# The last projection of a two-layer cross-attention with tokens on partitions: one kernel before and after the change

## The chip, the cores and the metric

The kernel runs on one core of one Trainium2 chip, in fp32. A core has five engines with instruction streams of their own: PE (TensorE, matrix products into PSUM), DVE (VectorE), ACT (ScalarE), POOL (GpSimd) and SP (SyncE, which here only issues DMA transfers). Each engine takes its instructions in order, and semaphores hold an instruction until what it needs from another engine or from a transfer is there. So an instruction that waits also holds everything behind it on its engine. The metric is the device time in microseconds, the median of several runs.

## What is computed

Two cross-attention layers, one after the other, on 8 batches of 100 tokens with 1024 features (`x`); each batch has a context of 1444 rows with 512 features.

```python
# layer 0
Q = query @ Wq + bq;  K = key @ Wk + bk;  V = key @ Wv + bv
weights = softmax(Q @ K^T * 1024**-0.5, axis=-1)        # over the keys
x = query + (weights @ V) @ Wo + bo
# layer 1
q = x @ Wq + bq;  k = ctx @ Wk + bk;  v = ctx @ Wv + bv
w = softmax(q @ k^T * 1024**-0.5, axis=1)               # over the queries
y = w @ v + x
mu, var = mean(y, -1), var(y, -1)
out = (y - mu) * rsqrt(var + 1e-6) * gamma + beta
```

In layer 1 the softmax runs over the query axis, so the weights of one query don't sum to one, and the bias `bv` enters a token's row multiplied by the sum of that token's weights. The kernel calls this sum `r`.

## The kernel before

**Layout.** The running activations are `xT`: features on partitions (8 chunks of 128) and all 800 tokens along the free dimension. Each layer forms, per batch, scores s with keys on partitions (12 chunks of 128, the last of 36 rows), the softmax, and A = context rows weighted by the softmax (512 features by 100 tokens). Values are never formed per key: A is projected afterwards by the value weights (`wv1`, 512 by 1024, in layer 1).

**What sets the order.** `alternated(b, ...)` (L1317) interleaves, on PE, the weighted rows A of batch b with the scores of batch b + 2, one step of each at a time: 48 steps, counted by n. When the scores of a batch are complete, its softmax (`softmax1`, L1128) is given out in pieces: DVE scales the scores and adds the key bias into `w`, takes the maximum over the tokens (`negmax`), ACT forms exponentials with their totals, DVE multiplies by the reciprocals, and POOL sums the weights over the keys (`weight_sums`, L1163). `LATER` says after how many pieces the rest of a softmax is put off until the next projection's code. DVE instructions between `vector.in_order = True` and `False` keep the order of the program; a scheduler places the others. The copy of a batch's A from PSUM to `A1T` is ACT's (L924).

**The second projection of layer 1.** `SETS` (L44) is batches 0 to 3, 4 to 6, and 7. After the A of a set's last batch, `project1` (L1197) multiplies with features on partitions: the weights are the stationary operand, the tokens (200 or 150 at a time) the moving one. It is a 2 by 2 block product with seven products in place of eight (X, Z, Y, W, reused and combined by additions); it needs four sums of weight blocks, made once by POOL (`project1_sums`, L1190), and four sums of token blocks, made by DVE for each set. Each product is 8 matmuls, and DVE adds the results into `xT`, where the residual already is.

**Finishing a batch.** `finish` (L1249) turns the batch's 100 columns of `xT` into token rows with 8 transposes on PE (`untransposed`, L1215 to L1232), DVE adds r times `bv` on the way out of PSUM into `z`, DVE takes mean and variance (`bn_stats`, `bn_aggr`), POOL raises the variance to -1/2, DVE forms (z - mean) * gamma, ACT scales, and POOL issues a transfer that adds `z` to the output, in which rows of beta have been written before: seven transfers by POOL (L1379) early in layer 1. `weight_totals` (L1179) gets r by transposing the sums of weights on PE and reducing on DVE. The dictionary `finished` (L1392) gives the batch and step n at which each is finished. `vectors` (gamma, beta and bv, repeated on all partitions, L1405 and after) are loaded after batch 3, into two of the ten buffers through which context tiles also stream.

**The end.** The last set is one batch. It is projected by `project_last` (L1263) with tokens on partitions in three pieces of columns; the first piece carries an extra column of row sums of the weights (`last_columns`, L1254, made by ACT), so that the mean is known early.

**Loads.** Context tiles (c, cT) come through SP's queue (`load_features`, `load_rows`), in the order of need, each when a buffer comes free.

Of the kernel before, what the change touches and what calls it, by code (L numbers as in the profile page):

```python
# [43 lines left out]
SETS = (range(0, 4), range(4, 7), range(7, 8))  # L44
LATER = {(1, 5): 4, (1, 7): 4}
# [10 lines left out]
def two_layer_cross_attention(ctx: ExitStack, tc: tile.TileContext, a: dict, out: bass.AP):  # L56
# [82 lines left out]
    prob = [feature_block(f"prob{n}") for n in range(3)]  # L139
    top = const.tile([P, P], F32, tag="top", name="top")  # L140
# [764 lines left out]
    def weighted_rows(s, layer, c, dst):  # L905
# [3 lines left out]
        for m in range(MC):  # L909
            r = max(keys(m), PAD)  # L910
            for k in range(LC):
                for h in both_sides():
                    nc.tensor.matmul(  # L913
                        ps[h * HP : (h + 1) * HP, k * T : (k + 1) * T],
                        c[m // CQ][:r, m % CQ, k * P + h * HP : k * P + (h + 1) * HP],
                        w[:r, m, :],
                        start=(m == 0 and k == 0),
                        stop=(m == MC - 1),
                        skip_group_check=True,
                    )  # L920
                if (m, k) == (MC - 1, LC - 1):
                    src = ps[:, :GT].rearrange("p (c t) -> p c t", t=T)
                    if layer:
                        nc.scalar.copy(dst, src)  # L924
                    else:
                        divided(s, ps, dst, src)
                yield

    def divided(s, ps, dst, src):
# [10 lines left out]
        r = work.tile([P, T], F32, tag="rrow", name=f"rrow_{s['b']}", bufs=2)  # L940
# [43 lines left out]
    def softmax0(s, groups, rest):  # L984
# [4 lines left out]
        most = work.tile([P, len(groups), T], F32, tag="most", name=f"most_{b}", bufs=1)  # L989
# [18 lines left out]
        shift = work.tile([P, P], F32, tag="shift", name=f"shift_{b}", bufs=1)  # L1008
# [154 lines left out]
    def weight_sums(s):  # L1163
# [4 lines left out]
        wsum = s["wsum"] = work.tile([P, T], F32, tag="wsum", name=f"wsum_{b}", bufs=6)  # L1168
# [10 lines left out]
    def weight_totals(pair):  # L1179

        n = P
        ps = bank(f"wsum_ps_{pair[0]['b']}")[:T, : 2 * n].rearrange("p (b n) -> p b n", n=n)
        for i, s in enumerate(pair):
            nc.tensor.transpose(ps[:, i, :], s["wsum"][:n, :], ident[:n, :n])
        r = small.tile([T, 2], F32, tag="r", name=f"r_{pair[0]['b']}", bufs=B // 2)
        nc.vector.tensor_reduce(r, ps, AX.X, ALU.add)
        for i, s in enumerate(pair):
            s["r"] = r[:, i : i + 1]

    def project1_sums(w):  # L1190
        t = weights.tile([P, LC, E], F32, tag="w", name="wv1_s")
        A = [[w[:, 2 * k + i, h * 512 : h * 512 + 512] for i in range(2)] for h in range(2) for k in range(2)]
        S = [[t[:, n, i * 512 : i * 512 + 512] for i in range(2)] for n in range(4)]
        left_sums(A, S, engine=nc.gpsimd)
        return A, S

    def project1(bs, A, S, At, between, room):  # L1197

        n, t0 = len(bs) * T // 2, bs[0] * T
        Bs = [[At[:, 2 * k + i, g * n : (g + 1) * n] for i in range(2)] for g in range(2) for k in range(2)]  # L1200
        sums = work.tile([P, LC, GT], F32, tag="gT", name=f"o1_{t0}_t", bufs=3).rearrange("p c t -> p (c t)")
        T_ = [[sums[:, (2 * k + i) * n : (2 * k + i + 1) * n] for i in range(2)] for k in range(4)]

        def add(r, g, banks):
            add_to_queries([4 * r + i for i in range(4)], t0 + g * n, n, banks)

        vector.in_order = True
        right_sums(Bs, T_)
        for _, steps in zip_longest(seven_products(f"o1_{t0}", A, Bs, S, T_, 4, n, add, add), room, fillvalue=0):
            for _ in range(steps):  # L1210
                next(between)
        run(between)
        vector.in_order = False

    def untransposed(s):  # L1215

        b = s["b"]  # L1220
        if b in range(3, 6):

            z = work.tile([P, LC, GT], F32, tag="gT", name=f"z_{b}", bufs=3).rearrange("p c t -> p (c t)")[:T, :E]
        else:
            z = row(f"z_{b}")[:T]
        s["z"] = z
        for j in range(2):
            ps = bank(f"z_{b}_{j}")
            for e in range(4):
                nc.tensor.transpose(ps[:T, e * P : (e + 1) * P], xT[:, 4 * j + e, b * T : (b + 1) * T], ident)  # L1230
            half = slice(j * 512, (j + 1) * 512)
            nc.vector.scalar_tensor_tensor(z[:, half], bv1[j][:T], s["r"], ps[:T, :], ALU.mult, ALU.add)  # L1232

    def normalise(s):
        b, z = s["b"], s["z"]
        stats = small.tile([T, 2, 6], F32, tag="stats", name=f"stats_{b}")
        for j in range(2):
            nc.vector.bn_stats(stats[:, j, :], z[:, j * 512 : (j + 1) * 512])
        mv = small.tile([T, 2], F32, tag="mv", name=f"mv_{b}")
        nc.vector.bn_aggr(mv, stats.rearrange("p a n -> p (a n)"))  # L1240
        rstd = small.tile([T, 1], F32, tag="rstd", name=f"rstd_{b}")
        nc.vector.tensor_scalar(rstd, mv[:, 1:2], EPS, None, ALU.add)
        nc.gpsimd.tensor_tensor(rstd, rstd, mhalf[:T], ALU.pow)  # L1243
        nc.vector.scalar_tensor_tensor(z, z, mv[:, 0:1], gamma[:T], ALU.subtract, ALU.mult)
        nc.scalar.activation(z, z, AF.Copy, scale=rstd)  # L1245

        nc.gpsimd.dma_start(out=out[b], in_=z, accum_op=ALU.add)

    def finish(s):  # L1249

        untransposed(s)
# [11 lines left out]
    def project_last(s, A, first):  # L1263
# [4 lines left out]
        z, centred = s["z"], row("centred")[:T]  # L1268
        n0 = first.shape[2] - 1
        parts = (slice(0, n0), slice(n0, n0 + 512), slice(n0 + 512, E))  # L1270
        unused = work.tile([P, L], F32, tag="half", name="unused", bufs=1)[:T]
        zs, sq = (small.tile([T, n], F32, tag=f"last{n}", name=f"last{n}") for n in (2, 3))
        mean, v, rstd = (small.tile([T, 1], F32, tag=n, name=n) for n in ("mean", "v", "rstd_last"))
# [4 lines left out]
        def scaled(part):  # L1278
            vector.tensor_tensor(z[:, part], centred[:, part], gamma[:T, part], ALU.mult)

        for j, part in enumerate(parts):
            n = part.stop - part.start
            ps = bank(f"ol_{j}")
            for k in range(LC):
                src = wv1[:, k, part] if j else first[:, k, :]
                m = src.shape[1]
                nc.tensor.matmul(ps[:T, :m], A[:, k, :T], src, start=(k == 0), stop=(k == LC - 1))
            if j == 0:
                vector.scalar_tensor_tensor(mean, ps[:T, n : n + 1], zs[:, 0:1], zs[:, 1:2], ALU.add, ALU.add)
                vector.tensor_scalar(mean, mean, 1.0 / E, None, ALU.mult)  # L1290
            vector.scalar_tensor_tensor(centred[:, part], ps[:T, :n], mean, z[:, part], ALU.subtract, ALU.add)
# [8 lines left out]
        nc.gpsimd.tensor_tensor(rstd, v, mhalf[:T], ALU.pow)  # L1300
        for half, queue in ((slice(0, E // 2), nc.sync), (slice(E // 2, E), nc.scalar)):
            vector.scalar_tensor_tensor(z[:, half], z[:, half], rstd, beta[:T, half], ALU.mult, ALU.add)
            queue.dma_start(out=out[B - 1][:, half], in_=z[:, half])
# [73 lines left out]
    for b in range(B - 1):  # L1377
        rows = a["L1_xattn_beta"].partition_broadcast(T)
        tc.keep_in_program_order(nc.gpsimd.dma_start(out=out[b], in_=rows))  # L1379
# [4 lines left out]
    cT = [list(load_features(0, parts=4)), list(load_features(1, (2,), 4))]  # L1384
    scores1 = scores_by_keys(batches[0], 1, cT[0], softmax1)
# [6 lines left out]
    finished = {(4, 2): 0, (4, 16): 1, (4, 30): 2, (5, 34): 3, (7, 2): 4, (7, 15): 5, (7, 28): 6}  # L1392
    totalled = {3: (0, 2), 6: (4,)}
    for bs in SETS:
        t = wide(f"A1T_{bs[0]}").rearrange("p c t -> p (c t)")[:, : LC * len(bs) * T]
        t = t.rearrange("p (c t) -> p c t", c=LC)
        for i, b in enumerate(bs):
            for n, _ in enumerate(alternated(b, 1, softmax1, t[:, :, i * T : (i + 1) * T])):
                if (b, n) in finished:
                    if (b, n) == (7, 28):  # L1400
                        weight_totals(batches[6:8])
                    finish(batches[finished[b, n]])
            if b == 1:
                AS = project1_sums(wv1)
            if b == 3:  # L1405
                vectors = [unit(f"vectors_{j}") for j in range(2)]
                gamma, beta = (v[:, :E] for v in vectors)
                bv1 = [v[:, E:] for v in vectors]
                for name, v in (("gamma", gamma), ("beta", beta)):
                    nc.gpsimd.dma_start(out=v, in_=a[f"L1_xattn_{name}"].partition_broadcast(P))  # L1410
                for j, v in enumerate(bv1):
                    nc.gpsimd.dma_start(out=v, in_=a["L1_xattn_bv"][j * 512 : (j + 1) * 512].partition_broadcast(P))
        if b == B - 2:
            first = last_columns(wv1)
        if b < B - 1:

            for first_of in totalled[b]:
                weight_totals(batches[first_of : first_of + 2])
            between, room = {3: (batches[5], (0, 2, 2, 2, 2)), 6: (batches[7], (1, 1, 1, 1, 2))}[b]
            project1(bs, *AS, t, between["softmax"], room)  # L1420
    untransposed(batches[B - 1])
    project_last(batches[B - 1], t, first)


# [22 lines left out]
```

## Time and profile before

Three runs: 588.76, 590.57 and 592.14 us, median 590.57.

| | us |
|---|---|
| profiled execution | 589.33 |
| its span | 587.6 |
| start of the first A of layer 1 | 414.0 |
| first set's projection | 479.7 to 499.2 |
| second set's projection | 545.4 to 559.8 |
| copies of A to A1T, batches 0 to 7 | 430.6, 446.8, 462.9, 479.6, 519.8, 537.8, 545.2, 572.4 |
| closing product starts | 572.9 |

Mean granted TensorE clock 0.997. The copies of A are a ruler for layer 1: between two of them lies a batch's A with the scores of a later batch, and whatever else stands there. The pairs that hold nothing else are 16.1 us apart. A chain of waits is followed back from the last instruction to what released each step; "issue" in it is time in which an engine waited for nothing that the profile shows.

### The profile page before, as it was taken

To read this page: it belongs to the slowest core of one execution; us is meant where nothing else is said; L and a number is where in the kernel's file an instruction comes from. 1 tells how busy PE (TensorE), PEld (TensorE's weight loads), DVE (VectorE), ACT (ScalarE), POOL (GpSimd) and SP (SyncE) were. 2 spreads that over 40 slices of the span, in tenths; PEclk is the share of its full clock that TensorE was granted. 3 is DMA by queue.
4 is the path that set the end of the run, shared out by engine and by line. 5 is a ranking of instruction groups with operands and counts; after the bars stand their busy time and mean duration, and the time that the engine had idled before them with its cause. 6 is when DMAs were issued, how large, how long until landed. Compare 5 with 4: busy or idle time off the path is not lost.

```text
span 587.6 us, 17570 instructions
## 1 busy us (share of the span) xinstructions
PE 575.2 (98%) x7470; PEld 497.6 (85%) x7470; DVE 399.6 (68%) x936; ACT 133.3 (23%) x349; POOL 135.0 (23%) x206
## 2 busy tenths in 40 slices
PE   9999999999999999999999899999999999999994
PEld 8887457678899999999998656787999999999992
DVE  1997579879686873876559587876444447664695
ACT  1331321433330112211111000103333303154313
POOL 3110110221111132241225000003922312341052
PEclk9999999999999999999999999999999999999998
DMA  8959989944599999999999605807889997599114
GB/s 274 308 107 321 311 202 296 287 73 97 94 248 360 332 378 365 369 371 366 370 316 289 134 0 206 301 2 222 281 289 304 338 314 258 158 310 328 40 30 85
DMA packets 74313, 142.96 MB, mean 243 GB/s; under 512 B 8572, under 2 KB 30332, under 8 KB 74236
## 3 DMA queue, kind: packets, MB, share of 16 engines
q1 hardware_dynamic: 65790, 117.81, 58.2%
q0 software_dynamic: 8048, 23.57, 19.7%
q8 instruction: 59, 0.97, 0.7%
q10 hardware_dynamic: 398, 0.47, 0.2%
q14 instruction: 18, 0.15, 0.1%
HBM read 124.40 MB, written 6.14 MB: 222 GB/s over the span
## 4 chain that ended last, share of the span: by engine, by line
PE 86%; DMA 6%; SPq 2%; issue 2%; POOL 2%; ACT 1%; DVE 0%; POOLq 0%; DVEq 0%
PE s L960 18%; PE A L913 17%; PE qk_x L166 7%; PE g_x L166 6%; PE o_x L166 5%; PE vo_x L166 4%; DMA cT<-in_ctxT 3%; PE o_y L166 3%; PE g_y L166 3%; DMA c<-in_ctx 3%; PE qk_z L166 2%; PE qk_y L166 2%; SPq L861 2%; PE o_w L166 1%; PE o_z L166 1%
## 5 line engine op out<-in xcount | busy, mean ns | idle before, releaser
L913 PE MATMUL A<-w,c 128*64 128x100 f32 (+1 forms) x3072 | 228.7, 249 | 1.7 <-issue 1.7
L913 PEld LDWEIGHTS A<-w,c 128*64 128x64 f32 (+1 forms) x3072 | 199.1, 137 | 3.6 <-issue 3.3
L960 PE MATMUL s<-g0T,cT 128*64 128x100 f32 (+1 forms) x1472 | 112.7, 249 | 2.0 <-issue 1.9
L960 PE MATMUL s<-g1T,cT 128*64 128x100 f32 (+1 forms) x1472 | 114.1, 249 | 0.1
L960 PEld LDWEIGHTS s<-g1T,cT 128*64 128x64 f32 (+1 forms) x1472 | 97.7, 136 | 2.6 <-issue 1.8
L960 PEld LDWEIGHTS s<-g0T,cT 128*64 128x64 f32 (+1 forms) x1472 | 96.8, 136 | 3.4 <-issue 2.7
L1172 POOL TENSOR_TENSOR part<-w 128x500 f32<-128x500 f32 x16 | 26.4, 1653 | 124.3 <-ACT w L1020 60.9
L1152 ACT ACTIVATE w<-w,negmax 128x100 f32<-128x100 f32 x96 | 35.0, 366 | 68.2 <-DVE negmax L99 68.2
L99 DVE SCALAR_TENSOR_TENSOR w<-s,kb 128x400 f32<-128x400 f32 (+2 forms) x32 | 13.9, 463 | 37.5 <-PE s L960 37.3
L1020 ACT ACTIVATE w<-w 128x400 f32<-128x400 f32 (+2 forms) x32 | 12.0, 442 | 120.3 <-DVE w L99 107.2
L99 DVE TENSOR_REDUCE most<-s 128x100 f32<-128x400 f32 (+1 forms) x24 | 12.5, 520 | 36.5 <-PE s L960 36.5
L166 PE MATMUL qk_x<-qk 128*128 128x256 f32 x128 | 31.0, 392 | 0.0
L166 PEld LDWEIGHTS qk_x<-qk 128*128 128x128 f32 x128 | 24.3, 198 | 3.3 <-ACT qk L440 0.2
L972 POOL MEMSET w<- 68x100 f32 x16 | 3.8, 237 | 75.3 <-PE A L913 36.4
L1232 DVE SCALAR_TENSOR_TENSOR z<-vectors,r,z 100x512 f32<-100x512 f32 x16 | 11.4, 743 | 11.8 <-PE z L1230 11.7
L99 DVE TENSOR_TENSOR w<-w,rtotal 128x400 f32<-128x400 f32 (+2 forms) x32 | 18.3, 570 | 1.1
L1245 ACT ACTIVATE z<-z,rstd 100x1024 f32<-100x1024 f32 x7 | 8.1, 1150 | 45.0 <-POOL rstd L1243 45.0
L1152 ACT ACTIVATION_READ_ACCUMULATOR w<-w,negmax 128x1 f32 x96 | 18.1, 188 | 0.0
L99 DVE TENSOR_TENSOR xT<-xT,o_x 128x400 f32<-128x400 f32 (+1 forms) x32 | 15.9, 538 | 2.8 <-PE o_x L166 2.4
L674 ACT ACTIVATE g1T<-g_x,k 128x400 f32<-128x400 f32 x4 | 2.4, 594 | 61.4 <-PE g_x L166 61.2
L578 POOL DMA_DIRECT2D qk_L_xattn_bk<-qk_L_xattn_bk x6 | 5.2, 922 | 47.8 <-DMA qk_L_xattn_bk<-qk_L_xattn_bk 18.9
L166 PE MATMUL vo_x<-vo 128*128 128x512 f32 x32 | 15.3, 595 | 0.0
(435 smaller groups left out, 1052.7 us busy)
## 6 DMA issues: line engine op xcount, KB each, us to landing
c<-in_ctx SPq DMA_DIRECT2D x176, 256.0 KB
cT<-in_ctxT SPq DMA_DIRECT2D x96, 176.0 KB
cT<-in_ctxT SPq DMA_DIRECT2D x32, 370.0 KB
cT<-in_ctxT SPq DMA_DIRECT2D x32, 352.0 KB
cT<-in_ctxT SPq DMA_DIRECT2D x32, 194.0 KB
vo<-in_L_xattn_Wo SPq DMA_DIRECT2D x8, 512.0 KB
qk<-in_L_xattn_WqT SPq DMA_DIRECT2D x8, 512.0 KB
qk<-in_L_xattn_WqT SPq DMA_DIRECT2D x15, 256.0 KB
```

The lines of the kernel that those rows point to most:

```text
L99: ins = getattr(nc.vector, op)(*args, **kw)
L166: nc.tensor.matmul(banks[n // per][:, n % per * width : (n % per + 1) * width], lhs[i][:, n * P : (n + 1) * P], rhs[i], start=(fresh and i ...
L578: nc.gpsimd.dma_start(out=to, in_=t, accum_op=ALU.add)
L861: tc.keep_in_program_order(nc.sync.dma_start(out=to, in_=src))
L913: nc.tensor.matmul(ps[h * HP : (h + 1) * HP, k * T : (k + 1) * T], c[m // CQ][:r, m % CQ, k * P + h * HP : k * P + (h + 1) * HP], w[:r, m, :],
L960: nc.tensor.matmul(to, cT[k][:, o : o + n], q[:, k, t0 : t0 + T], start=(k == 0 and m % GM == 0), stop=(k == LC - 1 or (k == LC - 2 and no ...
L972: nc.gpsimd.memset(s["w"][:PAD, MC - 1, :], 0.0)
L1020: nc.scalar.activation(rows, rows, AF.Exp)
L1152: nc.scalar.activation(rows[:, i, :], rows[:, i, :], AF.Exp, bias=negmax[:, i : i + 1], accum_out=total[:, i : i + 1])
L1172: add(part, w[:, 0:5, :], w[:, 5:10, :], ALU.add)
L1232: nc.vector.scalar_tensor_tensor(z[:, half], bv1[j][:T], s["r"], ps[:T, :], ALU.mult, ALU.add)
L1245: nc.scalar.activation(z, z, AF.Copy, scale=rstd)
```

## The change

The second projection of layer 1 is done with tokens on partitions. `TILES` cuts the 800 tokens into tiles of 128, 128, 112, 112, 96, 96 and 128, which don't follow the batches; three sets of two tiles are projected after batches 2, 4 and 6, and the last 128 tokens by `project_last`. A1T copies are split where a batch crosses a set's border. In a product the tokens are now the stationary operand and 512 columns of weights the moving one: two matmuls for a product. The token blocks' sums S and the weight blocks' sums T_ change sides, and the sums of weights are made by DVE at four given steps.

DVE turns the residual from `xT` into the token rows `z` in blocks of 32 by 32, 22 steps of four instructions, at steps listed in `at`; the last tile's alone is turned by PE (`turned_by_products`). The products are added to `z`. The sums of weights become r by matmuls of one column against ones, copied by ACT. Mean and variance come from two ACT passes with accumulation, whose elementwise output goes to the part of `xT` that is no longer needed. Beta's rows are written by six transfers on SP's queue, in order behind the layer's first context loads, in place of POOL's seven. The vectors are loaded after batch 1. `LATER` and the finishing steps are set anew; `wsums` is one tile for all batches, `rrow` has one buffer, and `shift` shares the buffer of `most`.

```diff
-SETS = (range(0, 4), range(4, 7), range(7, 8))
-LATER = {(1, 5): 4, (1, 7): 4}
+TILES = ((0, 128), (128, 128), (256, 112), (368, 112), (480, 96), (576, 96), (672, 128))
+SETS = ((2, (0, 1), range(0, 256)), (4, (2, 3), range(256, 480)), (6, (4, 5), range(480, 800)))
+LATER = {(1, 4): 4, (1, 6): 4}
...
+    wsums = work.tile([P, B * T], F32, tag="wsums", name="wsums", bufs=1)
...
-                        nc.scalar.copy(dst, src)
+                        for to, part in dst:
+                            nc.scalar.copy(to, src[:, :, part])
...
-        wsum = s["wsum"] = work.tile([P, T], F32, tag="wsum", name=f"wsum_{b}", bufs=6)
+        wsum = s["wsum"] = wsums[:, b * T : (b + 1) * T]
...
-    def weight_totals(pair):
...
-    def project1_sums(w):
...
-        left_sums(A, S, engine=nc.gpsimd)
...
+        B11, B21, B12, B22 = ([w[:, 2 * k : 2 * k + 2, h * 512 : h * 512 + 512]] for h in range(2) for k in range(2))
+        T_ = [[t[:, n, :].rearrange("p (i w) -> p i w", i=2)] for n in range(4)]
...
+        def steps():
+            for n in range(4):
+                vector.in_order = True
+                right_sums((B11, B21, B12, B22), T_, (n,))
+                vector.in_order = False
+                yield
+
...
+    def project1(pair, Bs, T_, t, more):
+        A11, A21, A12, A22 = ([t[:, 2 * k : 2 * k + 2, g * n : g * n + n]] for k in range(2) for g in range(2))
...
+        def product(ps, lhs, rhs, fresh):
+            for i in range(2):
+                nc.tensor.matmul(
+                    ps[:n, :],
+                    lhs[0][:, i, :],
+                    rhs[0][:, i, :],
+                    start=(fresh and i == 0),
+                    stop=(i == 1),
+                    skip_group_check=True,
+                )
+
+        def add(g, c, ps):
+            to = pair[g]["z"][:n, c * 512 : c * 512 + 512]
+            vector.tensor_tensor(to, to, ps[:n, :], ALU.add)
...
+        left_sums((A11, A12, A21, A22), S)
+        X = bank("o1_x")
+        product(X, A11, B11, True)
+        add(0, 0, X)
+        Z = bank2("o1_z")
+        product(Z, A12, B21, True)
+        add(0, 0, Z)
+        weight_totals((*pair, *more))
+        Y = bank("o1_y")
+        product(Y, S[0], T_[0], True)
+        add(1, 1, Y)
+        for s in more:
+            turned_by_products(s)
+        product(X, S[1], T_[1], False)
+        add(0, 1, X)
+        W = bank2("o1_w")
+        product(W, A22, T_[3], True)
+        add(1, 0, W)
+        product(X, S[2], T_[2], False)
+        add(1, 0, X)
+        add(1, 1, X)
+        product(Y, S[3], B22, False)
+        add(0, 1, Y)
...
+    def weight_totals(some):
+
+        ps = bank("totals")
+        for i, s in enumerate(some):
+            n = s["n"]
+            nc.tensor.matmul(ps[:n, i : i + 1], wsums[:, s["t0"] : s["t0"] + n], ones[:, :1], start=True, stop=True)
+            s["r"] = small.tile([P, 1], F32, tag="r", name=f"r_{s['t0']}", bufs=len(TILES))[:n]
+            nc.scalar.copy(s["r"], ps[:n, i : i + 1])
+
+    def turned_blocks(some):
+
+        for i, s in enumerate(some):
+            if i == 3:
+                z = work.tile([P, LC, GT], F32, tag="gT", name=f"z_{i}", bufs=3).rearrange("p c t -> p (c t)")[:, :E]
+            else:
+                z = row(f"z_{i}")
+            s["z"] = z
+            to = z.rearrange("p (c q i) -> p q c i", q=P // QD, i=QD)
+            for t in range(0, s["n"], QD):
+                vector.in_order = True
+                for q in range(P // QD):
+                    src = xT[q * QD : (q + 1) * QD, :, s["t0"] + t : s["t0"] + t + QD]
+                    vector.transpose(to[t : t + QD, q, :, :], src)
+                vector.in_order = False
+                yield
...
+    def turned_by_products(s):
+
+        t = slice(s["t0"], s["t0"] + s["n"])
+        s["z"] = work.tile([P, LC, GT], F32, tag="gT", name="z_last", bufs=3).rearrange("p c t -> p (c t)")[:, :E]
+        banks = [bank(f"z_last_{j}") for j in range(2)]
+        for e in range(EC):
+            nc.tensor.transpose(banks[e // 4][:, e % 4 * P : (e % 4 + 1) * P], xT[:, e, t], ident)
+        add_value_bias(s, s["z"], banks)
...
-            nc.vector.bn_stats(stats[:, j, :], z[:, j * 512 : (j + 1) * 512])
-        nc.vector.bn_aggr(mv, stats.rearrange("p a n -> p (a n)"))
...
+        nc.scalar.activation(unused, src, AF.Copy, accum_out=total)
+        nc.scalar.activation(less, total, AF.Copy, scale=-1.0 / E)
+        nc.scalar.activation(unused, src, AF.Square, bias=less, accum_out=squares)
+        vector.in_order = True
+        vector.tensor_scalar(rstd, squares, 1.0 / E, EPS, ALU.mult, ALU.add)
+        vector.scalar_tensor_tensor(z, z, less, gamma[:n], ALU.add, ALU.mult)
...
-        nc.gpsimd.dma_start(out=out[b], in_=z, accum_op=ALU.add)
+        nc.gpsimd.dma_start(out=result[t0 : t0 + n], in_=z, accum_op=ALU.add)
...
+        z = s["z"]
+        vector.in_order = True
+        add_value_bias(s, z, [z[:, j * 512 : (j + 1) * 512] for j in range(2)])
+        vector.in_order = False
...
-    for b in range(B - 1):
-        rows = a["L1_xattn_beta"].partition_broadcast(T)
-        tc.keep_in_program_order(nc.gpsimd.dma_start(out=out[b], in_=rows))
...
+    n = TILES[-1][0] // 6
+    for i in range(6):
+        loaded_in_order(result[i * n : (i + 1) * n], a["L1_xattn_beta"].partition_broadcast(n))
...
-    finished = {(4, 2): 0, (4, 16): 1, (4, 30): 2, (5, 34): 3, (7, 2): 4, (7, 15): 5, (7, 28): 6}
+    finished = {(3, 34): 0, (4, 10): 1, (5, 22): 2, (5, 34): 3, (7, 4): 4, (7, 16): 5}
+    at = {b: (4, 16, 28, 40) for b in range(3, 6)} | {0: (12, 36), 1: (4, 20, 36), 2: (4, 16, 28), 6: (4, 20)}
+    sums_at = ((0, 46), (1, 12), (1, 28), (2, 10))
...
+        for n, _ in enumerate(alternated(b, 1, softmax1, parts)):
+            if n in at.get(b, ()):
+                next(turned, None)
+            if (b, n) in sums_at:
+                next(more_sums)
+            if (b, n) in finished:
+                finish(tiles[finished[b, n]])
+        if b == 1:
+            vectors = [unit(f"vectors_{j}") for j in range(2)]
+            gamma, beta = (v[:, :E] for v in vectors)
+            bv1 = [v[:, E:] for v in vectors]
+            for name, v in (("gamma", gamma), ("beta", beta)):
+                nc.gpsimd.dma_start(out=v, in_=a[f"L1_xattn_{name}"].partition_broadcast(P))
+            for j, v in enumerate(bv1):
+                nc.gpsimd.dma_start(out=v, in_=a["L1_xattn_bv"][j * 512 : (j + 1) * 512].partition_broadcast(P))
+        for last, pair, _ in SETS:
+            if b == last:
+                project1([tiles[i] for i in pair], Bs, T_, homes[b], tiles[6:] if b == 6 else ())
+                if b + 2 < B:
+                    run(batches[b + 2]["softmax"])
...
-    untransposed(batches[B - 1])
-    project_last(batches[B - 1], t, first)
+    project_last(tiles[6], homes[6][:, :, TILES[6][0] - SETS[2][2].start :], first)
```

## The prediction

> **What bounds the kernel now.** I read the page's totals and slices first, then the waits by engine, then the chain of waits, then groups of instructions by shape, and last the timeline of the end.
>
> ```profile
> span 587.6 us, 17570 instructions
> PE 575.2 (98%) x7470; PEld 497.6 (85%) x7470; DVE 399.6 (68%) x936; ACT 133.3 (23%) x349; POOL 135.0 (23%) x206
> PE   9999999999999999999999899999999999999994
> PE 86%; DMA 6%; SPq 2%; issue 2%; POOL 2%; ACT 1%; DVE 0%; POOLq 0%; DVEq 0%
> ```
>
> TensorE (PE) is busy in 98% of the span; no slice but the last is under 8. So the kernel is bound by PE's sum of work, and whatever is taken off PE is gained, as long as nothing makes PE wait. The waits by engine say how little waiting there is (time, times, longest):
>
> ```profile
> PE s L960 <- issue: 1.9, 3, 0.7
> PE A L913 <- issue: 1.7, 1, 1.7
> PE warm L111 <- DVE ones L108: 1.1, 1, 1.1
> ```
>
> One wait of 1.7 us stands out, with no releaser. The chain of waits places it at 327.09, and prices the work that is replaced:
>
> ```profile
> 327.09 1.65 issue
> 459.72 10.00 DMA cT<-in_ctxT
> 471.55 3.96 DMA cT<-in_ctxT
> 480.30 2.71 PE o_x L166 x16
> 500.43 1.01 PE z L1230 x8
> 545.56 2.04 PE o_x L166 x16
> ```
>
> A product of the second projection is 2.71 us in the first set (8 matmuls of 200 columns, two records each: 339 ns) and 2.04 us in the second (150 columns, 255 ns); one batch's transposes for the residual are 1.01 us. The two DMA steps show that the loads of batch 3 arrived just in time. Prices of DVE and POOL, by shape:
>
> ```profile
> L596 DVE STREAM_TRANSPOSE qk_L_xattn_bk<-qk_L_xattn_bk 128x1024 f32<-128x1024 f32 x2 | 2.5, 1234 | 0.0
> L1238 DVE BATCH_NORM_STATS2 stats<-z 100x6 f32<-100x512 f32 x14 | 8.9, 680 | 0.0
> L1232 DVE SCALAR_TENSOR_TENSOR z<-vectors,r,z 100x512 f32<-100x512 f32 x16 | 11.4, 743 | 11.8 <-PE z L1230 11.7
> ```
>
> The end, in the timeline: the last copy of weighted rows, then the closing product, then 14.7 us from its start to the span's end.
>
> ```profile
> 572.38 0.47 ACT L924 COPY A1T<-A 128x400 f32<-128x400 f32 x1
> 572.90 2.82 PE L1287 MATMUL ol<-wv_first,A1T 128*100 128x384 f32 x8
> ```
>
> [...] In fp32 here a 32x128 transpose took 300 ns, 512 elements 696 and 1024 elements 1234: time goes with the elements of one partition. [...] POOL's first step of the weight sum (part, L1172) took 1.27 us at 202.59, by DVE transposes, and 6.03 us at 246.72, by DVE additions of two SBUF tensors. [...]
>
> **The change part by part.** Times below are in the profiled execution (589.33 us, span 587.6); it is 1.24 below the median of 590.57, so I form a difference there and add it to the median.
>
> PE's arithmetic. A 512-column fp32 matmul is 0.859 us (eight of vo_z took 6.87). The sets before: 7 x 2.71 + 7 x 2.04 = 33.3. After: three sets of 14 matmuls, 3 x 12.03 = 36.1, so +2.8. Seven of the eight transpose groups go. By the timeline, in A(4), which held three, PE took 20.58 us from copy to copy where a pair without them takes 16.13; 4.45 more; A(5), with one, took 17.97, 1.84 more; A(7), with three and 0.43 of weight totals, took 12.07 where A(6) alone took 8.24, 3.4 more. That is 9.7 for seven, 1.4 each, of which 1.01 is the work. One group of eight stays, for the last tile, so six are saved ahead of the end of A(7), -8.4; the eighth of before, 1.08 at 571.88, stood behind it, beside the A1T copy. The weight totals by transposes (0.57 for four, twice, -1.1) become seven one-column matmuls (+0.6). Sum: -6.1 for the end of the last A, if PE never waits.
>
> DVE's arithmetic. It gets 22 steps of 4 transposes of 256 elements. By the slope between the 128-, 512- and 1024-element rows one is 433 ns, with the start of the next 440: 88 x 0.44 = 38.7 us. No row has this mix of strides and partition offsets; bounds are 0.30 (the 32x128 row) and 0.60. It also gets the four sums of weights (4 x 1.22 = 4.9, formerly POOL's) and loses 14 bn_stats (9.5 us) and seven aggregates. ACT gets, for each of six tiles, two passes over 1024 columns with accumulation (about 1.06 + 0.19 each) and a small one (0.29): 2.8 us. Both engines have room on average (DVE 68%, ACT 23%), so the question is only what stands ahead of a softmax in the order, because DVE and ACT run in order, and PE waits in the projection for the softmax's sums.
>
> I walked through the order of after's instructions with these durations. Regular period: 16.13 us for a batch's A and the scores two batches on; with T the copy at its end, the next softmax's first DVE step is at T - 2.97, its last at T + 4.95, and POOL's weight sum is done at T + 9.2.
>
> Set 0 (batches 0 to 2, starts 462.75). X and Z need the first tile only. The second total waits for ACT's copy of the first, which stands behind exponentials: +0.65. Length 12.03 + 0.17 + 0.65 = 12.85.
>
> Set 1. Ahead of softmax 6 DVE has 16 transposes (7.1), two bias steps (1.4), the wait for ACT's statistics of tile 1 (2.8), and the scaling (1.43): 12.7 us from the end of softmax 5 at 496.8, to 509.6, where the softmax could have begun at 505.0. Softmax 6 is 4.5 late. Behind it on DVE are the sums of A1T that product Y needs, and on ACT the copy of the first total, which holds the second total matmul. PE, done with X and Z at 511.4, waits to about 515.7: +4.3. Length 16.5.
>
> Set 2. Ahead of softmax 7 stand tiles 2 and 3, finished one after the other: last additions, two statistics rounds, and between them ACT's copy and sums of the weight columns (1.47 and four of about 1.2); DVE reaches the softmax at about 543 where 537.6 was possible. Its weight sum, which the total of the last tile needs, comes at 555; PE is there at 552.2: +2.7. Length 12.03 + 0.26 + 1.4 + 2.7 = 16.4.
>
> Sum from 462.75: 12.85 + 2 x 16.13 + 16.5 + 16.13 + 8.24 + 16.4 + 8.2 = 110.6, to 573.3. Before, the last A ended at 571.87. The last A1T copy then stands on ACT behind the statistics of tiles 4 and 5: additions end at about 565.9, bias 1.4, statistics 2.8, rstd 0.8, scale 1.15, statistics 2.8: 574.9. The closing product starts about 575.4 in place of 572.90: +2.5. Its tail, 14.7, has the same operations on 128 rows in place of 100: no change.
>
> Beta's rows. Before, seven POOL transfers issued at 317.46 landed to 333.9, and PE's unexplained 1.65 us falls among them, together with an instruction-fetch transfer at 326.24 that came 16.6 us after its predecessor (usually 5 to 6). After, six transfers of 459 KB stand in SP's ring ahead of later loads, at about 366 to 385; DMA was idle there from 382 to 396. I count -1.65, bounds 0 and -2. They delay the loads of batch 2 by up to 13.6 us, which the idle stretch absorbs: c2 needed at 414 now lands around 394 to 400.
>
> The vectors (gamma, beta, bv: 1.5 MB, and two of ten stream buffers for good) move from 456 to about 425. In before they cost the stream 6.2 us, and batch 3's loads had nothing to spare. Batch 2's had 8.6 to 11.5 us; with 6.2 gone and fewer buffers about 2 us stay. Cost 0, bounds 0 and +4.
>
> Net: +2.5 - 1.65 = +0.85, and 590.57 + 0.85 = 591.4 us.
>
> **The rivals.** A, the walk above: the PE time saved is nearly all given back by three waits for softmaxes that stand behind longer DVE and ACT work. For it: the exact order; against: a walk by mean durations adds up queues that may overlap.
>
> B, the waits are small. If transposes take 0.30 us, set 1's 16 are 2.2 us shorter; if ACT's passes and DVE's finishes overlap the softmax's own waits, most of 0.65 + 4.3 + 2.7 goes. With sets 1 and 2 unhindered A ends at 566.3, and the ACT queue moves up with it, leaving about 1.6 of its wait: closing product at 568.4, -4.5, with beta's -1.65: 584.4 us. For it: PE's 98% and the low ACT share; against: four instructions in a row in DVE's order.
>
> C, slower: loads late in A(2). From 425 on, two buffers fewer and the vectors' 6.2 us meet batch 2, whose slack was 8.6; if the slack is used up, PE waits by the excess, and nothing later wins it back, since the sets only follow. At 4 us of excess, 595.4 us. It decides when the excess passes 2.1 us, since 591.4 + 2.1 is the bound of what can be told from no change. For it: batch 3's waits in the chain of before; against: 15 us of idle DMA just ahead.
>
> D, beta's rows have nothing to do with the 1.65 us: A becomes 593.1 us; I leave that in A's spread.
>
> **How the numbers follow.** What a measurement of this kernel can tell from no change is about 0.5%, 2.95 us. A gets 0.38 (0.08 faster, 0.21 within, 0.09 slower, by its spread of about 3.5 us), B 0.36 (0.35 and 0.01), C 0.26 (0.24 slower, 0.02 within). So faster 0.43, within 0.24, slower 0.33. The forecast is A's. A's own range is 588 to 595; cases of both signs hold most of the chance, so the whole range goes from 583 (B with all waits gone) to 597 (C with the stall at 327 kept).
>
> **What would show it.** Right: PE's busy time near 567 to 569; PE waits of about 4 us in set 1 and 2 to 3 us in set 2, by r or o_t; the transposes near 430 ns; the last A1T copy waiting on ACT, not on PE; no gap at 327. Wrong: PE waits in A for c or cT near 446 to 462 (C), or no wait over 1 us in the sets (B).

## The result, and the profile after

The changed kernel takes 593.89 us in the median of 10 runs (592.42 to 595.96); the kernel before took 589.77 in its 10 runs beside it. The ratio is 1.0062, 95% interval 1.0041 to 1.0083, so the change costs about 3.7 us. The forecast was 591.4, a rise of 0.85 us: the direction and the range (583 to 597) held, the size did not.

The page of the changed kernel, to be laid beside the one of before (PEclk is the granted TensorE clock in tenths, 40 slices):

```profile
span 591.8 us, 17217 instructions
PE 572.7 (97%) x7280; PEld 474.6 (80%) x7280; DVE 426.5 (72%) x987; ACT 147.8 (25%) x387; POOL 121.7 (21%) x189
PE   9999999999999999999999999999999999699985
PEclk9999999999999999999999999999999999899998
```

PE's busy time fell by 2.5 us only, and the span grew by 4.2: PE waits more. Most of it happens in the slice from 503 to 518 us (the 6), and in the same slice the clock falls. The waits of PE (total, times, longest):

```profile
PE totals L1253 <- ACT r L1255: 5.7, 3, 4.8
PE ol L1351 <- ACT A1T L927: 2.4, 1, 2.4
...
PE totals L1253 <- POOL wsums L1181: 0.7, 1, 0.7
PE A L915 <- issue: 0.2, 1, 0.2
```

The 1.7 us wait of A is gone; in its place stand 5.7 us for r, 2.4 for the last copy of A and 0.7 for the sums of weights, three waits that the prediction had named. Set 1 in the timeline (start, duration; in brackets the idle time before it and its releaser):

```profile
501.84 0.15 DVE L100 TENSOR_SCALAR rstd<-squares 128x1 f32<-128x1 f32 x1 [2.73 <-ACT xT L1300]
...
504.56 4.05 DVE L100 STREAM_TRANSPOSE z<-xT 32x256 f32<-32x256 f32 x9
...
508.32 1.88 PE L1209 MATMUL o_z<-wv,A1T 128*112 128x512 f32 x4
508.64 0.63 DVE L100 SCALAR_TENSOR_TENSOR w<-s,kb 128x300 f32<-128x300 f32 x2
...
514.41 0.38 ACT L1156 ACTIVATE w<-w,negmax 128x100 f32<-128x100 f32 x1 [0.15 <-DVE negmax L100]
...
514.79 0.14 ACT L1255 COPY r<-totals 112x1 f32<-112x1 f32 x1
...
515.07 0.50 PE L1253 MATMUL totals<-ones,wsums 128*112 128x1 f32 x2 [4.76 <-ACT r L1255]
...
515.44 3.34 PE L1209 MATMUL o_y<-wv_s,o_t 128*112 128x512 f32 x4
```

Read it backwards: the second totals matmul waits for ACT's copy of r, which stands behind an exponential, which waits for DVE's maximum, which waits for softmax 6 to start at 508.64, which stands on DVE behind transposes and, ahead of them, behind tile 1's finishing: there DVE stood still for 2.73 us until ACT's statistics were there. And product Y, two matmuls that take 1.9 us elsewhere, takes 3.34. A window there, and two at the closing product (window and its length, PE busy with the count of instructions, granted clock, DMA share, GB/s):

```profile
514.84:518.26 3.42, 3.19 (x6) 0.50 1.06 306
...
572.87:576.28 3.41, 1.03 (x17) 1.00 0.52 62
576.28:579.70 3.42, 3.42 (x7) 0.50 0.27 53
```

About the end of each of these two waits the granted clock falls to 0.50, for 3.41 us. The end in the timeline:

```profile
574.26 1.15 ACT L1300 ACTIVATE xT<-z,less 96x1024 f32<-96x1024 f32 x1
...
575.40 0.47 ACT L927 COPY A1T<-A 128x400 f32<-128x400 f32 x1
...
575.93 4.54 PE L1351 MATMUL ol<-wv_first,A1T 128*128 128x384 f32 x8 [2.38 <-ACT A1T L927]
```

The copy of the last A stands behind ACT's statistics of tile 5, and the closing product's first piece takes 4.54 us where it took 2.82 before.

### The profile page after: what moved, and what is told of

The parts are those of the page before. It is cut to its first block, busy times and chain, and to the rows that moved or that the text cites. A ratio compares the mean times of both kernels' runs of the same rounds, so it can differ in the third digit from the quotient of the medians.

```text
span 591.8 us, 17217 instructions
## 1 busy us (share of the span) xinstructions
PE 572.7 (97%) x7280; PEld 474.6 (80%) x7280; DVE 426.5 (72%) x987; ACT 147.8 (25%) x387; POOL 121.7 (21%) x189
## 5 line engine op out<-in xcount | busy, mean ns | idle before, releaser
L915 PEld LDWEIGHTS A<-w,c 128*64 128x64 f32 (+1 forms) x3072 | 197.1, 137 | 3.0 <-issue 2.1
L963 PEld LDWEIGHTS s<-g1T,cT 128*64 128x64 f32 (+1 forms) x1472 | 96.0, 136 | 2.5 <-issue 1.9
L100 DVE STREAM_TRANSPOSE z<-xT 32x256 f32<-32x256 f32 x88 | 38.3, 435 | 1.3
L1305 POOL TENSOR_TENSOR rstd<-rstd,mhalf 128x1 f32<-128x1 f32 (+2 forms) x6 | 9.2, 1537 | 44.0 <-DVE rstd L100 44.0
L1179 POOL TENSOR_TENSOR part<-part 128x100 f32<-128x100 f32 x32 | 15.5, 484 | 2.5
L100 DVE TENSOR_TENSOR w<-w,rtotal 128x400 f32<-128x400 f32 (+2 forms) x32 | 15.2, 480 | 0.8
L1298 ACT ACTIVATE xT<-z 128x1024 f32<-128x1024 f32 (+2 forms) x6 | 6.3, 1055 | 36.4 <-DVE z L100 36.4
```

What stands on the lines that cost most here:

```text
L100: ins = getattr(nc.vector, op)(*args, **kw)
L915: nc.tensor.matmul(ps[h * HP : (h + 1) * HP, k * T : (k + 1) * T], c[m // CQ][:r, m % CQ, k * P + h * HP : k * P + (h + 1) * HP], w[:r, m, :],
L963: nc.tensor.matmul(to, cT[k][:, o : o + n], q[:, k, t0 : t0 + T], start=(k == 0 and m % GM == 0), stop=(k == LC - 1 or (k == LC - 2 and no ...
L1179: add(part[:, 0, :], part[:, 0, :], more, ALU.add)
L1298: nc.scalar.activation(unused, src, AF.Copy, accum_out=total)
L1305: nc.gpsimd.tensor_tensor(rstd, rstd, mhalf[:n], ALU.pow)
```

## The experiments

Every ratio is to the kernel before, with its 95% interval; the changed kernel has 1.0062. Unless it is said otherwise an edit is made in the changed kernel.

**Beta's rows back on POOL (e1).**

```diff
-        loaded_in_order(result[i * n : (i + 1) * n], a["L1_xattn_beta"].partition_broadcast(n))
+        tc.keep_in_program_order(nc.gpsimd.dma_start(out=to, in_=rows))
...
     wv1 = weights.tile([P, LC, E], F32, tag="w", name="wv1")
```

> The changed kernel with beta's rows written by POOL again, in six transfers at the place where the kernel before issues its seven. Theory 1 (beta's transfers cause the PE wait near 327 us): the wait returns, the first A of layer 1 starts near 406 instead of 403.4 us, and the time is 1.7 to 2.6 us above the changed kernel's 593.9: about 596. Rival (the lead comes from elsewhere, as from POOL's load of wv1 or from how instruction fetches fall): the first A stays near 403.4 and the time stays near 593.9.

Measured: 597.92 us, ratio 1.0110 (1.0071 to 1.0148). Its waits near 327 us, and two windows, of which the first holds the longest wait:

```profile
PE A L915 <- issue: 3.2, 2, 2.4
```

```profile
327.24:330.65 3.41, 1.57 (x22) 1.00 1.04 215
330.65:334.07 3.42, 3.42 (x7) 0.50 0.09 26
```

The wait is back, 2.36 us at 326.7, and the clock falls behind it. The time between two fixed points of layer 0's projection (first o_z_x to first o_w_x) is 33.03 us in the changed kernel, 35.03 in the kernel before and 37.42 here. A 16 KB instruction transfer comes at 320.58 in the changed kernel and at 326.24 in the kernel before; whether PE's wait hangs on that transfer no run shows. The first theory, that beta's transfers cause the wait, stands, with more than the cost that was expected: 4.0 us in place of 1.7 to 2.6.

**PE kept busy in its waits (e2).**

```diff
+        Y = bank("o1_y")
+        fill = 5 if pair[0]["t0"] == 256 else 0
+        weight_totals((*pair, *more), lambda: [product(Y, A11, B11, True) for _ in range(fill // 2)])
...
+            for _ in range(3 if j == 0 else 0):
+                nc.tensor.matmul(ps[:, :384], ident, first[:, 0, :], start=True, stop=True)
```

> The changed kernel with matmuls whose results are overwritten, to keep PE busy while it waits: four of 512 columns ahead of the second totals matmul of set 1, three of 384 columns ahead of the closing product. No wait is shortened. Theory 1 (after a wait of some us PE runs at a lower granted clock): product Y of set 1 falls from 3.34 to about 1.9 us, the closing product's first piece from 4.54 to about 2.8 us, granted clock near 1.00 in both, time 2.6 to 3.1 us less: about 591. Rival (Y and the closing product are long because their operands arrive late): both keep their length and the time stays near 593.9.

Measured: 593.44 us, ratio 1.0051 (1.0025 to 1.0076), not told apart from the changed kernel: the gain of 2.6 to 3.1 us that was expected did not come. Its profiled span is 589.8, 2.0 less, but by its device time (592.44 against 593.56) that execution is 1.1 faster, and the medians are 0.45 apart. The mechanism shows all the same: Y takes 1.95 us and the closing piece about 2.85, both at a clock of 1.00, so the clock and not late operands had made them long. But:

```profile
PE o_x L1209 <- DVE z L100: 2.0, 1, 2.0
```

In set 1 a new wait of 2.0 us stands three products further on: X has to be added to z by DVE before it is written again, and DVE is still at softmax 6. The slow Y had only hidden it, and set 1 gains nothing: it lasts 19.6 us in place of 19.1. At the close, where nothing else is late, the time from the closing product to the end of the span is 14.2 us in place of 15.9.

**The totals ahead of the copies of r (e3).**

```diff
             nc.tensor.matmul(ps[:n, i : i + 1], wsums[:, s["t0"] : s["t0"] + n], ones[:, :1], start=True, stop=True)
+        for i, s in enumerate(some):
+            n = s["n"]
             s["r"] = small.tile([P, 1], F32, tag="r", name=f"r_{s['t0']}", bufs=len(TILES))[:n]
             nc.scalar.copy(s["r"], ps[:n, i : i + 1])
```

> The changed kernel with all totals matmuls of a set ahead of ACT's copies of r, so that no totals matmul waits for a copy. If the wait of 4.77 us in set 1 comes from the copies' place behind the exponentials, it shrinks to what product Y needs of its sums of tokens on DVE, 512.0 instead of 515.1: 3 us less, a wait of about 1.7 us, no fall of the clock (another 1.4 us), so about 589.5. Rival (softmax 6 late on DVE is the cause in any form): the wait only changes its name, to o_t, and stays over 4 us; about 593.5.

Measured: 590.13 us, ratio 0.9994 (0.9969 to 1.002).

```profile
PE totals L1253 <- POOL wsums L1181: 2.2, 1, 2.2
...
PE o_y L1209 <- DVE o_t L100: 1.7, 1, 1.7
...
PE o_x L1209 <- DVE z L100: 0.9, 1, 0.9
```

This is near what was expected. The wait for r was a wait of its own: what is left of it is the 1.7 us for DVE's sums that were expected, and the 0.9 of X. The clock in set 1 stays at 1.00. Softmax 7 is now the later of the two in set 2 (2.2).

**Tile 1's second half behind softmax 6 (e4).**

```diff
     nc.scalar.activation(unused, src, AF.Square, bias=less, accum_out=squares)
+    yield
...
     finished = {(3, 34): 0, (4, 10): 1, (5, 22): 2, (5, 34): 3, (7, 4): 4, (7, 16): 5}
+    scaled = {(3, 34): 0, (5, 1): 1, (5, 22): 2, (5, 34): 3, (7, 4): 4, (7, 16): 5}
```

> The changed kernel with the second half of finishing tile 1 (DVE's rstd, its subtraction of the mean and scaling, POOL's power, ACT's scale, the output) put off from step (4, 10) to step (5, 1), so that it stands behind softmax 6 on DVE and not ahead of it. My theory: softmax 6 starts at about 504.5 instead of 508.6, the wait for r in set 1 falls from 4.8 to under 1 us and the clock doesn't fall, about 5 us less in set 1; softmax 7 becomes about 1.4 us later, so up to 1.5 of it is given back in set 2: about 590. Rival (the wait for r is a matter of ACT's queue alone): softmax 6 earlier, but the wait stays above 3 us; about 593.

Measured: 589.98 us, ratio 0.9989 (0.9968 to 1.001). Set 1 lasts 13.5 us in place of 19.1, set 2 17.9 in place of 15.0. The wait of set 2, then the window behind it:

```profile
PE totals L1253 <- POOL wsums L1181: 1.9, 1, 1.9
```

```profile
552.64:556.05 3.41, 3.41 (x10) 0.50 0.00 0
```

The two waits for r in sets 0 and 1 are 1.2 us together. So some 4.1 us of DVE's in-order stream (a wait for ACT's statistics of 2.7 and two steps), placed ahead of the softmax, were behind 5.6 of the 6.3 us by which set 1 is longer than the 12.85 it takes in e6. What came back in set 2 is 2.9 us, not 1.5: the wait of 1.9 took the clock with it.

**The close (e5).** The second halves of tiles 4 and 5 go behind the last A, and ACT's copy ahead of their two scales.

```diff
+    run(*(ends[i] for i in (4, 5)))
     project_last(tiles[6], homes[6][:, :, TILES[6][0] - SETS[2][2].start :], first)
```

> The changed kernel with the second halves of finishing tiles 4 and 5 (rstd, scaling, power, ACT's scale, output) put behind the last A, and ACT's copy of the last A ahead of their two scales. In the changed kernel the closing product waits 2.38 us for that copy. Theory 1 (the copy waits for ACT's statistics and scale of tile 4, 1.15 us, behind a 1.5 us power on POOL): the wait falls from 2.4 to 0.2 to 0.6 us, time about 2 us less, about 592. Rival (statistics of tile 5 alone keep ACT late): the wait stays above 1.5 us, under 1 us gained.

Measured: 591.10 us, ratio 1.0012 (0.9992 to 1.0031), with

```profile
PE ol L1356 <- ACT A1T L927: 0.6, 1, 0.6
```

The wait falls as the first theory said, and the time falls by 2.8 us, a little more than expected.

**Vectors after batch 2 (e7).** `if b == 1:` becomes `if b == 2:`.

> The changed kernel with gamma, beta and bv loaded after batch 2 in place of batch 1. If their early loading cost nothing, as the trace of the changed kernel says (no wait of PE for c or cT), the time is the same, 593 to 595, or a little more where batch 3's loads have no slack. If it cost PE time in A(1) or A(2): the gap of 0.55 us at 433.2 goes, 0.5 to 1 us less.

Measured: 593.65 us, ratio 1.0066 (1.0044 to 1.0089). The gap at 433.2 goes, and the stretch from 403.5 to set 0 takes 56.7 us in place of 57.3, but the time doesn't change by an amount that can be told. The early load isn't what makes the changed kernel slow.

**Beta alone in the kernel before (e8).** Seven transfers on SP's queue, in the same place as in the change.

```diff
+    for b in range(B - 1):
+        loaded_in_order(out[b], a["L1_xattn_beta"].partition_broadcast(T))
```

> The kernel before with one part of the change alone: beta's seven transfers taken from POOL near 317 us and put on SP's queue behind the first context loads of layer 1. Theory (they delay PE's instructions there, as the run with beta back on POOL says): no PE wait near 327, the first A of layer 1 at about 403.5 instead of 406.0, ratio to the kernel before 0.995 to 0.997. Rival (the wait needs something else of the kernel before too, or SP's loads of batch 2 and 3 become late by it): the ratio stays within 0.998 to 1.003.

Measured: 586.88 us, ratio 0.9925 (0.9904 to 0.9946): more than expected. What PE still waits for in an A is

```profile
PE A L913 <- issue: 0.3, 1, 0.3
```

The wait near 327 is gone, the distance of the two fixed points is 33.03 again, so 2.0 us of the 4.4 are seen in the profiles. In e1 the same stretch cost 4.4. Where the rest of e8's gain lies no trace shows, but the clock on record points the same way: its mean is 0.9943 over the 25 runs of the kernel before beside e8, and 0.9969 over the 16 of e8. Over 589 us that is 1.5 us. The profiled execution of the kernel before, at 0.997, lost no clock at 327; that of e1, at 0.989, did.

**Two edits together (e9).** e3 and e4 in one kernel.

> The changed kernel with the two edits for sets 0 and 1 together: totals matmuls ahead of the copies, and tile 1's second half behind softmax 6; softmax 7 and the close are left as they are. If both edits cure the same wait of set 1, the two gains don't add: waits of set 1 near 0 and of set 0 gone, but softmax 7 still late, so 2 us of wait in set 2 and 2.4 at the close: 588 to 590, ratio to the kernel before 0.996 to 0.999. Rival (the gains add): about 586.

Measured: 585.95 us, ratio 0.9915 (0.9882 to 0.9948): the rival's number. In the medians the gains add (0.0068 with e3, 0.0073 with e4, 0.0147 with both). In set 1 they don't, and there the theory holds: 19.1 us in the changed kernel, 15.9 in e3, 13.5 in e4, 12.9 with both. What that leaves short comes back in set 2, where e4 lost 2.9 us and both edits together 1.0. No wait is left in sets 0 and 1; 2.2 us in set 2 and 2.4 at the close remain, as expected, but here neither lowers the clock.

**Everything together (e6).**

```diff
-    finished = {(3, 34): 0, (4, 10): 1, (5, 22): 2, (5, 34): 3, (7, 4): 4, (7, 16): 5}
+    finished = {(3, 34): 0, (4, 10): 1, (5, 10): 2, (5, 22): 3, (7, 4): 4, (7, 16): 5}
+    scaled = {(3, 44): 0, (5, 1): 1, (5, 33): 2, (6, 1): 3}
```

with e3's and e5's edits; tiles 4 and 5 end as in e5.

> The changed kernel with everything that was found put together: totals matmuls ahead of the copies of r, each finish cut in two with transposes or a softmax between the halves (tile 1's second half behind softmax 6, tile 3's behind softmax 7), and the closing copy ahead of the last two scales. No work is left out. If the waits, and not the work that DVE and ACT took over, are what the change lost: waits in the three sets under 1.5 us together, none over 0.6 us ahead of the closing product, clock near 1.00 throughout; 593.9 - 4.8 - 0.6 - 0.5 - 2.0 - 1 to 3 of clock = about 583 to 585, faster than the kernel before. Rival (DVE or ACT is too full, so a wait removed comes back at the next place): time above 588.

Measured: 582.91 us, ratio 0.9870 (0.9847 to 0.9894). That is just below the expected 583 to 585. Its page and its waits:

```profile
PE 569.6 (98%) x7280; PEld 473.0 (81%) x7280; DVE 425.9 (73%) x987; ACT 148.2 (25%) x387; POOL 122.6 (21%) x189
...
PEclk9999999999999999999999999999999999999999
```

```profile
PE s L965 <- issue: 1.8, 3, 1.0
...
PE A L915 <- issue: 1.0, 2, 0.9
PE ol L1358 <- ACT A1T L927: 0.6, 1, 0.6
PE s L965 <- DMA cT<-in_ctxT: 0.5, 1, 0.5
```

No wait is left in the three sets, with the same 88 transposes, the same sums and the same passes of ACT (DVE 425.9, ACT 148.2 us busy). So the change was slow by the order of its work and not by the amount of it.

## Why the prediction was right, and where it was too small

The direction is in part luck. A rise of 0.85 us lies inside the 2.95 that the prediction called no change, and its own chances put faster (0.43) above slower (0.33). Two of its terms missed in opposite ways: with the 4.4 us that e8 measured for beta's move in place of 1.65, its sum would have come to -1.9, and what it left out, above all the fall of the clock (some 3 us in the profile), made the measured change a rise again.

**PE's arithmetic: nearly right.** PE's busy time was put at 567 to 569. The page says 572.7, but some 3 us of that is slow clock (1.4 in Y, 1.7 at the close); where the clock is full, in e6, it is 569.6, just above the range.

**DVE's arithmetic: right.** The transposes were put at 433 ns and the bounds were not needed. The row of the changed kernel:

```profile
L100 DVE STREAM_TRANSPOSE z<-xT 32x256 f32<-32x256 f32 x88 | 38.3, 435 | 1.3
```

**The waits: right in place and cause.** Set 0: 0.65 forecast, 0.55 measured. Set 1: 4.3 and 4.8, with softmax 6 beginning 12.9 us after softmax 5 has ended, where the walk had 12.7. Set 2: 2.7 and 1.1, because PE came there later than the walk said, being late already. The close: the copy behind tile 5's statistics, 2.1 and 2.4. One price in that queue was wrong: rstd was put at 0.8 us, and POOL's power takes 1.53.

**Beta: right in cause, too small.** The step counted -1.65, the length of the wait. The stretch is 2.0 us shorter, and e1 and e8 show that the gain can be 4.4. A wait was priced at its length, and in e1 it cost more, as the clock fell behind it. One reading was off: the 16.6 us between two instruction transfers were held against a usual 5 to 6, but at this place the changed kernel, with no wait there, has 11.9.

**The vectors: right.** Rival C falls: PE waits for no c or cT in the changed kernel, and for 0.5 us at most in any experiment, and e7 gains nothing that can be told.

**The step that was mis-sized** is "Its tail, 14.7, has the same operations on 128 rows in place of 100: no change", and with it set 1's "Length 16.5". The tail has the same operations, and it takes 15.9 us, because the wait ahead of it lowers PE's clock; where the clock stays up it takes 14.1 to 14.5, with a shorter wait (e2, e6) and with the same 2.4 us of wait (e1, e3, e4, e9). Set 1 took 19.1: of the 2.6 us more, 0.5 is the wait itself, 1.4 the slow Y (or, with a fast Y, the 2.0 us wait of X for DVE, which the walk had also left out), and some 0.65 the set's own length, which is 12.85 in e6 where the walk had 12.2. The clock on record for every run says the same: its mean is 0.991 over the changed kernel's 10 runs and 0.995 over 42 runs of the kernel before, some 2 us of 590. From the first A of layer 1 to the closing product the kernel lost 5.6 us, where 2.5 was forecast; with 1.2 more in the tail and 2.6 gained ahead of layer 1, that is the 4.2 us between the two profiled spans.

**Rival B** (small waits) was wrong for the changed kernel and near to what the same work takes in a better order: 584.4, and e6 measured 582.9. Part of the nearness is chance, as B's sum holds beta's move at 1.65 too.

**What the change was worth in parts.** Beta's move alone gives 0.9925. The rest of the change, in the order it came in, takes the kernel from there to 1.0062, some 8 us; in the order of e6 it takes it to 0.9870, some 3 us faster than beta's move alone, with intervals that don't touch (up to 0.9894, and from 0.9904).

## What to carry to other kernels

When work moves from the busiest engine to the others, write out what then stands ahead of each instruction that the busiest engine waits for; an in-order engine with 28% of idle time can still be 4 us late at one place. In this kernel an instruction that waits for another engine (DVE's rstd for ACT's statistics) was better put a stage later than the work it waits for (e4: 589.98 us in place of 593.89; e6, with the other edits: 582.91), and a small copy out of a PSUM tile did not belong between two matmuls that write to that tile (e3: 590.13). In this kernel a wait of TensorE of about 2 us or more was to be priced above its length: four of eleven waits of 1.9 to 2.4 us met a fall of the clock to 0.50 (at the close of the changed kernel 4.54 us of work where 2.82 is the length at 1.00), and so did the waits of 4.8, 4.6 and 4.8 us in set 1 of the changed kernel, e1 and e7.

## What was not expected of the hardware

In the traces of the kernel before and of the changed kernel the clock on record is 1.00 or 0.50 and nothing between. Under work the changed kernel has it at 0.50 from 514.84 to 518.26 and from 576.28 to 579.70, 3.413 us each; the two starts lie 61.44 us apart, 18 times as much. In e1 from 330.65 and in e4 from 552.64 it is at 0.50 for 3.42 and 3.41 us (the windows above). In set 1 of e1 and e7 the clock is at 0.50 for longer, at least 3.7 us (520.3 to 524.0 and 515.0 to 518.7).

The clock fell at waits shorter than 3.41 us too, but not at all of them. Waits of 4.8, 4.6 and 4.8 us in set 1 of the changed kernel, e1 and e7 met a slow stretch. Of eleven waits of 1.9 to 2.4 us four did: the close of the changed kernel and of e7 (2.4 each), 2.36 us at 326.7 in e1, 1.89 in set 2 of e4; the same close with 2.4 us stayed at 1.00 in e1, e3, e4 and e9, and so did set 2 of e3 and e9 with 2.2 and X in e2 with 2.0. The closes of the changed kernel and of e1 differ in where the wait falls. In the changed kernel the wait of 2.38 us lies within one window of 3.41 us and leaves 1.03 us of work in it (the line from 572.87 above). The same wait in e1 lies across the border of two, which keep 2.64 and 1.81 us of work:

```profile
576.41:579.83 3.42, 2.64 (x62) 1.00 0.00 0
579.83:583.24 3.41, 1.81 (x6) 1.00 0.78 115
```

Cut into windows of 3.413 us from the first point of the clock's record (7.14 us in the kernel before, 6.26 in the changed kernel), the two traces give 170 and 171 windows. Each window with 1.03 us of PE work or less (580.58 in the kernel before; 511.43, 572.87 and 586.53 in the changed kernel) is followed by a clock of 0.50, and each with 1.68 us (583.11 in the changed kernel) or more by 1.00. In e1 the window with 1.57 us at 327.24 is followed by 0.50. So the line for this kernel is, as an estimate from the 1.57 and 1.68 us, with ends of matmuls that are modelled, 1.7 to 1.8 us of idle time in a window of 3.41. The closing piece under a slow window took 1.7 us more (4.54 for 2.82).

Under POOL's transfers of beta's rows PE stood still for 1.65 us in the kernel before and 2.36 us in e1 with nothing in the profile but "issue". In the kernel before, a 16 KB instruction transfer comes there 5.7 us later than in the changed kernel (326.24 and 320.58). The same rows from SP's queue, at a time when PE has fewer instructions (81 matmul records in the 19 us from 366 in the changed kernel, where the 10 us from 317 have 203), led to no such wait of PE in e8, where 0.3 us of "issue" is left in A. Whether the queue or the time makes the difference was not tried.
